# Swin block and dynamic depthwise convolution: the prologue of a long kernel reordered (raw means for folded weights, deviations between shift products, rows turned by DMA, zeroing on ScalarE)

## The chip, the cores and the metric

The kernel runs on one core of one Trainium2 chip. The metric is the device time of one run in microseconds, the median of several runs. Everything, prologue and weights included, happens in one launch.

## The reference, cut to what matters

Sixteen images of 192 channels and 56 x 56 pixels go through two layers. The first is a Swin block with shifted windows, the second a depthwise convolution whose taps are computed from the image's own channel means.

```python
# layer 0; x: (16, 192, 56, 56) float32, tokens are pixels
h = layernorm(x over channels) * norm1_g + norm1_b
h = roll(h, (-3, -3));  win = 7 x 7 windows of h          # 64 windows an image
q, k, v = win @ qkv_w + qkv_b                             # 192 -> 3 x 6 heads x 32
attn = softmax((q * 32**-0.5) @ k.T + rel_bias[REL_IDX] + mask)
x1 = x + roll_back((attn @ v) @ proj_w + proj_b)
y = layernorm(x1) * norm2_g + norm2_b
x2 = x1 + gelu(y @ fc1_w + fc1_b) @ fc2_w + fc2_b         # 192 -> 768 -> 192
# layer 1
t = relu(batchnorm(mean(x2 over pixels) @ w1.T))          # 192 -> 48
taps = (t @ w2.T + b2) * causal_mask                      # 4 taps a channel and image
out = depthwise3x3(x2, taps) + bias
```

## The kernel before, in words

**Tiles.** A step `i` is two window rows of an image, one from its upper and one from its lower half: 2 x 7 x 56 = 2 x 392 tokens. There are 4 steps an image and 64 in all. `x0` holds channels 0 to 127 of a whole image on 128 partitions; `x1` holds channels 128 to 191, the upper half of the image on partitions 0 to 63 and the lower on 64 to 127. An image is loaded already rolled.

**Layer norms without a mean.** The mean over channels is never subtracted from the tokens. The weights (`wqkv`, `wf1`) carry the norm's gamma and are centred instead, so that each output's weights add up to zero over the input channels; beta times the weights is added to the bias. A token is only multiplied by its inverse deviation, a *dv*. For that, `norm_squares` (L258) squares a step, `norm_stats` sums values and squares on TensorE (`st` in PSUM) with the selector `sel`, `norm_vars` and `norm_root` make variance and root, VectorE takes the reciprocal, and `norm_spread` (L350 on) writes the few rows to DRAM as `rows` and reads each back onto 128 partitions (`dv`, L366, on the SP queue). `norm1_scale` (L391, L399) multiplies and writes the windows `win`; `norm2_scale` (L413 to L419) does the same for the MLP's input `yn`. In the loop the stats come folded (`norm_folded`): two `xs` copies by DMA on SP bring halves side by side, GpSimd adds sums (L293, L295), squares are taken (L302, L309), and GpSimd adds the squares up (L314, L315).

**Attention of a step.** `attention_qk` makes `pq`, `pk` and `pe` and copies them out as queries `q4`, `q2` and as block-diagonal keys `kbd`, whose other entries stay zero from the prologue. `attention_v` makes `pv`; `attention_v_out` (L524) copies it into `vbd`, two buffers used in turn with zeros between heads, by block: half 0 by VectorE, half 1 by ScalarE. `attention_scores` gives, by window pair, `sc` on TensorE; `top` adds the table `bias_t` (L552, L559, position bias and mask) on VectorE and takes the exponent (L562) on ScalarE; `share` makes sums and quotients (L566 to L568, the last on GpSimd into `prob`). `attention_turn` transposes `prob` (`pt`, `prt`), `attention_values` gives `po`, `attention_rows` `o`, `project` `pp`, `residual` (L651, L657) adds it to `x`.

**The MLP.** `mlp_first` is fc1 and gelu (`ph`, L671), with callbacks `after` and `between` (the latter holds the `st` products of other steps); `mlp_wide`, `mlp_narrow` and `mlp_out` (L717) are fc2 (`pf`).

**Order.** Each engine executes what the program writes for it in that order[...]. PSUM is four pairs of banks, given out by hand with `banks(name, k)`. All matmuls go through the helper `mm` (L87). The loop body works on the convolution of an earlier image, the MLP of step `i-2`, the attention of step `i`, and queries and norms of later steps. Ahead of the loop a prologue (L853 to L1134) builds the weights and runs steps 0, 1 and part of 2 as pieces. All of the change lies in this prologue and in its helpers.

**The pieces of the prologue that the change touches**, in TensorE's order: `st_a` (stats of step 0), `fq_m` (means of the scaled qkv weights, by `fold_means`), `qkb_p` (`shift`: beta times the raw weights, one row), `dv` (step 0's two deviations spread by matmul), six one-row products that turn the `qkb` row into columns (`turn_row`), `st_b` (steps 1 and 2), step 0's `pq` to `pv`, scores `sc`, `pb_p` (fc1's shift row, turned by six more products, and small ones for the projection's bias), step 1's `pq`, and so on to `ff_m` (fc1's means), `st_c`, step 0's MLP and the loop. On VectorE: `fold_scale` (L158, L160) makes ten scaled copies of the qkv weights, `fold_center` subtracts the means, and `biases` (L911) builds four quarters of `bias_t`, 24 additions. On GpSimd and VectorE: the zeroing of `kbd`, `vbd` and `prob`. On SP: the loads of `x` and of the weights, one after the other.

Of the kernel before, what the change touches and what calls it, by code (L numbers as in the profile page):

```python
# [8 lines left out]
F32 = mybir.dt.float32  # L9
AF = mybir.ActivationFunctionType  # L10
ALU = mybir.AluOpType
# [8 lines left out]
N = WS * WS  # L20
# [16 lines left out]
def tile_swin_then_dynamic_conv(  # L37
# [48 lines left out]
    def mm(dst, lhs, rhs, start, stop):  # L86
        nc.tensor.matmul(dst, lhs, rhs, start=start, stop=stop, skip_group_check=True)  # L87
# [33 lines left out]
    def rows2(dst, src, queue):  # L121

        for h in range(2):
            queue.dma_start(dst[h * 64 : h * 64 + 64], src[C0:DIM])

    def columns_load(sources, tag, name, queue):
        n = sum(count for _, count in sources)
        rows = one.tile([n, 256], F32, tag=tag, name=f"{name}_rows")
        at = 0
        for src, count in sources:  # L130
            queue.dma_start(rows[at : at + count, 0:DIM], src.rearrange("(r c) -> r c", c=DIM))
            at += count
        return rows, n, name
# [17 lines left out]
    def fold_scale(raw, g, dst, groups, engine=nc.vector):  # L151
        for to, lo, n, factor in groups:
            for c in range(2):
                d, r = dst[:, c, to : to + n], raw[:, c, lo : lo + n]
                if engine is nc.scalar:
                    nc.scalar.activation(d, r, AF.Copy, scale=g[c])
                elif factor == 1.0:
                    nc.vector.tensor_scalar(d, r, g[c], None, ALU.mult)  # L158
                else:
                    nc.vector.tensor_scalar(d, r, g[c], factor, ALU.mult, ALU.mult)  # L160
# [15 lines left out]
    def shift(dst, raw, n, be, name):  # L176


        for c in range(2):
            cs = slice(c * n // 2, (c + 1) * n // 2)  # L180
            mm(dst[:, c, : n // 2], be[0].broadcast_to([128, 128]), raw[:, 0, cs], True, False)
            mm(
                dst[:, c, : n // 2],
                be[1][0:64].broadcast_to([64, 128]),
                raw[0:64, 1, cs],
                False,
                True,
            )
        row = one.tile([1, 2, n // 2], F32, tag="xs", name=name)
        nc.scalar.copy(row, dst[0:1, :, : n // 2])  # L190
        return row.rearrange("o c n -> o (c n)")

    def turn_row(dst, row, lo, n):
        mm(dst, row[:, lo : lo + n], ident[0:1, 0:1], True, True)
# [10 lines left out]
    qkb = const.tile([128, 3], F32, tag="qkb", name="qkb")  # L205
    wp0 = const.tile([128, DIM], F32, tag="wp0", name="wp0")
# [3 lines left out]
    f1b = const.tile([128, NFC], F32, tag="f1b", name="f1b")  # L210
    wf2 = const.tile([128, NFC, DIM], F32, tag="wf2", name="wf2")
# [27 lines left out]
    mask_t = one.tile([PW, 2, 2, N], F32, tag="prt", name="mask_t", bufs=4)  # L239
# [104 lines left out]
    def norm_vars(keys, st, tag="dev"):  # L344

        lo, hi = min(keys) * 32, max(keys) * 32 + 32
        d = one.tile([128, T], F32, tag=tag, name=f"dev_{keys[min(keys)]}")
        part = d[64 + lo : 64 + hi]
        nc.scalar.activation(part, st[lo:hi, 0, :T], AF.Square)
        nc.vector.tensor_tensor(part, st[64 + lo : 64 + hi, 0, :T], part, ALU.subtract)  # L350
        return part, d
# [4 lines left out]
    def norm_spread(keys, part, tags=("dv1", "sq01"), order=(1, 0)):  # L356

        rows = dram.tile([2 * len(keys), T], F32, tag="rows", name=f"rows_{keys[min(keys)]}")
        nc.sync.dma_start(rows, part[::16])
        out = {}  # L360
        for side in order:
            if side not in keys:
                continue
            v = one.tile([128, 2, T], F32, tag=tags[side], name=f"dv_{keys[side]}")
            at = 2 * (side - min(keys))
            nc.sync.dma_start(  # L366
                v,
                rows[at : at + 2].rearrange("(o h) t -> o h t", o=1).broadcast_to([128, 2, T]),
            )
            out[side] = v  # L370
        return out
# [61 lines left out]
    def attention_qk(i, kq, ke, kk, between=None, evac=nc.scalar, early=None, k_too=False):  # L433
# [34 lines left out]
        def biased(dst, src, b):  # L468
            if evac is nc.vector:
                nc.vector.tensor_scalar(dst, src, b, None, ALU.add)  # L470
            else:
                nc.scalar.activation(dst, src, AF.Identity, bias=b)

        def e(a):
            biased(q2[a * 64 : a * 64 + 64], pe[0:64, a, :T], qkb[0:64, 2:3])
            for h in range(2):
                p = slice(64 + h * HD, 64 + (h + 1) * HD)
                g = a * 2 + h
                biased(
                    kbd[g * HD : (g + 1) * HD, 2, :, h, :],  # L480
                    pe[p, a, :T].rearrange("p (w t) -> p w t", t=N),
                    qkb[p, 2:3],
                )
# [29 lines left out]
    def attention_v_out(pvs):  # L513

        for blk, pv in enumerate(pvs):
# [347 lines left out]
    for h in range(4):  # L863
        nc.vector.memset(pick[h * HD : (h + 1) * HD, h % 2 : h % 2 + 1], 1.0)
# [12 lines left out]
    load_rows(*images[0], 0, 3 * WS, HALF, nc.sync)  # L877
    nc.sync.dma_start(rawf[:, 0], fc1_w[0:C0])
    rows2(rawf[:, 1], fc1_w, nc.sync)
# [9 lines left out]
    nc.sync.dma_start(mask_t, win_mask)  # L889
# [15 lines left out]
    def biases(r, e):  # L905
        for half in range(2):
# [15 lines left out]
    nc.vector.memset(kbd, 0.0)  # L922
    norm_squares("1_0", 0, 0, nc.scalar, ("yn0", "q4"))
    fold_scale(
        raw,
        g1,
        wqkv,
        (
            (0, 0, 128, SCALE),
            (128, DIM, 128, 1.0),  # L930
            (256, 128, 64, SCALE),
            (320, DIM + 128, 64, 1.0),
            (384, 2 * DIM, DIM, 1.0),
        ),
    )
# [3 lines left out]
    part, _ = norm_vars(keys, st, "o")  # L939
    norm_root(part)  # L940
    nc.vector.reciprocal(part, part)
    norm_squares("1_1", 1, 0, nc.scalar)
    pm = fold_means(wqkv, 3 * DIM, "fq", 0)
    pq = banks("qkb_p", 2)
    row = shift(pq, raw, 3 * DIM, be1, "qkb_row")
    pq = pq[:, 0, 384:390]
    norm_squares("1_2", 2, 1, nc.scalar)

    pd = banks("dv_0", 3)
    for h in range(2):  # L950
        pick_row = ident[64:96, 64 + h * 16 : 65 + h * 16].broadcast_to([32, 128])
        mm(pd[:, h, :T], pick_row, part, True, True)
    fold_center(wqkv, 3 * DIM, pm)
# [8 lines left out]
    for _, c, at, lo, n, _ in parts:  # L962
        turn_row(pq[at : at + n, c : c + 1], row, lo, n)
    g2, be2, f2b, pb, cb = columns(*rows3, 1, nc.scalar.copy)
    norm1_scale(0, pd[:, :, :T], nc.vector)
    for dst, c, at, _, n, b in parts:
        nc.vector.tensor_tensor(dst, b, pq[at : at + n, c : c + 1], ALU.add)
    nc.vector.tensor_scalar(qkb[:, 0:1], qkb[:, 0:1], SCALE, None, ALU.mult)
    nc.vector.tensor_scalar(qkb[0:64, 2:3], qkb[0:64, 2:3], SCALE, None, ALU.mult)
    nc.vector.tensor_scalar(kb, pick, qkb[:, 1:2], None, ALU.mult)  # L970
# [4 lines left out]
    norm_stats(keys, {0: 1, 1: 2}, st)  # L975
    part, _ = norm_vars(keys, st)
    norm_root(part)
# [4 lines left out]
    for r in range(2):  # L982
        for e in range(2):
            biases(r, e)
# [11 lines left out]
    for t in (*vbd, *prob):  # L996
        nc.gpsimd.memset(t, 0.0)
# [9 lines left out]
    fold_scale(rawf, g2, wf1, ((0, 0, HID, 1.0),), nc.scalar)  # L1007
    norm1_scale(1, dvs.pop(0), nc.gpsimd)
    w2v = w2.rearrange("(c t) r -> c t r", t=9)[:, 0:NTAP, :]
    b2v = b2.rearrange("(c t) -> c t", t=9)[:, 0:NTAP]  # L1010
    nc.gpsimd.dma_start(w2n[:, 0], w2v[0:C0])
    nc.gpsimd.dma_start(b2t[:, 0], b2v[0:C0])
    rows2(w2n[:, 1], w2v, nc.gpsimd)
    rows2(b2t[:, 1], b2v, nc.gpsimd)
    nc.gpsimd.dma_start(wf2, fc2_w.rearrange("(f p) n -> p f n", p=128))
# [4 lines left out]
    pbp, f1p, pt = pv[:, 0, 384:386], pv[:, 0, 392 : 392 + NFC], pv[:, 1, 384:512]  # L1020
    top(0)
    row = shift(pv, rawf, HID, be2, "f1b_row")

    def rows_to_columns():
        for f in range(NFC):
            turn_row(f1p[:, f : f + 1], row, f * 128, 128)

    qs[1], outs = attention_qk(1, 2, 0, 1, rows_to_columns, nc.vector)
# [19 lines left out]
    share(3)  # L1048
    for c in range(2):
        nc.vector.tensor_tensor(pb[c], pb[c], pbp[:, c : c + 1], ALU.add)  # L1050
    nc.vector.tensor_tensor(f1b, f1b, f1p, ALU.add)
# [6 lines left out]
    outs[3]()  # L1058
    o = attention_rows(0, attention_values(0, prts, 3, 2))
# [16 lines left out]
    pm = fold_means(wf1, HID, "ff", 1)  # L1076
    top(2)
    residual(0, pp, pair1)
# [17 lines left out]
    dvs.update(norm_spread(keys, part))  # L1096
# [9 lines left out]
    v_whole()  # L1106
    copies, sums_, squares, fold = norm_folded("1_4", 4, 0)
    copies()
    squares(nc.scalar)()
    table(AF.Gelu)  # L1110
    sums_((0,))
    yns[0] = norm2_scale(0, dvs.pop(1), True)
    sums_((1,))
    fold()
    attention_v_out(pvs)
# [245 lines left out]
```

## Time and profile before

| | |
|---|---|
| median of 3 runs | 3045.67 us (3045.51 to 3046.77) |
| profiled run | 3046.2 us; span 3044.4 us |
| mean granted TensorE clock | 0.998 |
| TensorE busy | 3022.7 us of 3044.4, 25174 products |
| VectorE, ScalarE, GpSimd busy | 2156.3, 1948.7, 1343.5 us |
| span of the prologue on TensorE, first `st` product of the MLP at | 104.75 us |

PE is TensorE's matmul, PEld its weight load, DVE VectorE, ACT ScalarE, POOL GpSimd, SP the queue engine. TensorE is idle for some 22 us in all. A group's line reads: engine, operation, result<-operands, shape, count, then the time in brackets for which the engine stood idle ahead of it and what released it. Times at the left of a timeline are microseconds from the start of the span. Lines L87 are all matmuls, so they are told apart by the tile's name.

### The profile page before, as it was taken

How to read it: one execution, taken by the hardware profiler on the slowest of the kernel's cores; microseconds unless marked ns; L12 is line 12 of the kernel's file. 1: busy time of each engine (PE TensorE's matmuls, PEld its weight loads, DVE VectorE, ACT ScalarE, POOL GpSimd, SP SyncE). 2: the span in 40 equal slices, each digit the busy share in tenths (PEclk: the TensorE clock that was granted, in tenths of full speed). 3: DMA queues.
4: the chain of work that ended last, by engine and by line, in shares of the span. 5: the costliest groups of instructions: out<-in, count | busy, mean ns of one | idle time of the engine just before them, and what ended most of it. 6: DMA issues, size and time to landing. Idle time of an engine off the chain costs nothing.

```text
span 3044.4 us, 62149 instructions
## 1 busy us (share of the span) xinstructions
PE 3022.7 (99%) x25174; PEld 1891.4 (62%) x25174; DVE 2156.3 (71%) x3841; ACT 1948.7 (64%) x3159; POOL 1343.5 (44%) x1269
## 2 busy tenths in 40 slices
PE   9999999999999999999999999999999999999998
PEld 5666666666666666666666666666666666666654
DVE  8656677676686676776866867767767668668664
ACT  4666676666666666766766667667666667666563
POOL 6444534444435445344444444453454444444422
PEclk9999999999999999999999999999999999999999
DMA  4112121111211112121121211212111121211101
GB/s 111 33 31 59 41 75 41 43 60 46 73 38 62 52 44 68 44 72 36 41 67 47 70 36 52 65 41 78 39 47 56 46 73 38 62 52 43 33 30 56
DMA packets 68711, 159.89 MB, mean 53 GB/s; under 512 B 11250, under 2 KB 35288, under 8 KB 66504
## 3 DMA queue, kind: packets, MB, share of 16 engines
q1 hardware_dynamic: 66766, 153.84, 16.7%
q8 instruction: 199, 3.26, 0.4%
q0 software_dynamic: 1360, 1.26, 0.3%
q14 instruction: 88, 0.72, 0.1%
q10 hardware_dynamic: 298, 0.81, 0.1%
HBM read 92.24 MB, written 38.93 MB: 43 GB/s over the span
## 4 chain that ended last, share of the span: by engine, by line
PE 97%; DVE 1%; DMA 1%; POOL 1%; issue 0%; ACT 0%; SPq 0%; POOLq 0%; DVEq 0%; ACTq 0%
PE ph L87 26%; PE pf L87 25%; PE pv L87 8%; PE pp L87 8%; PE po L87 6%; PE pq L87 5%; PE pt L581 5%; PE sc L87 4%; PE pk L87 4%; PE pe L87 4%; PE st L87 2%; PE pc L87 0%; DMA wp<-in_L_conv_proj_w_dram 0%; PE pb_p L87 0%; DVE e L559 0%
## 5 line engine op out<-in xcount | busy, mean ns | idle before, releaser
L87 PE MATMUL pf<-hid,wf 128*128 128x392 f32 (+1 forms) x3072 | 802.6, 493 | 1.5 <-DVE e L552 1.5
L87 PE MATMUL ph<-yn,wf 128*128 128x392 f32 (+1 forms) x3072 | 799.3, 497 | 1.8 <-ACT vbd L524 1.5
L568 POOL TENSOR_TENSOR prob<-e,tot 113x588 f32<-113x588 f32 x256 | 298.3, 1176 | 1098.8 <-DVE tot L567 1098.6
L87 PEld LDWEIGHTS ph<-yn,wf 128*128 128x128 f32 (+1 forms) x3072 | 426.4, 188 | 346.6 <-issue 47.5
L87 PEld LDWEIGHTS pf<-hid,wf 128*128 128x128 f32 (+1 forms) x3072 | 386.2, 164 | 301.3 <-issue 120.2
L524 ACT COPY vbd<-pv 49x192 f32<-49x192 f32 x512 | 160.5, 313 | 575.9 <-DVE vbd L524 571.4
L717 DVE SCALAR_TENSOR_TENSOR x<-pf,cols,x 128x784 f32<-128x784 f32 (+1 forms) x128 | 106.2, 830 | 506.3 <-PE pf L87 447.6
L671 ACT ACTIVATE hid<-ph,f1b 128x784 f32<-128x784 f32 x384 | 337.2, 913 | 133.7 <-PE ph L87 132.2
L781 DVE SCALAR_TENSOR_TENSOR y<-x,wt,y 128x770 f32<-128x770 f32 x282 | 287.7, 1030 | 15.3 <-ACT y L773 7.0
L87 PEld LDWEIGHTS pv<-wqkv,win 64*128 64x128 f32 (+1 forms) x2048 | 255.4, 188 | 31.4 <-issue 1.2
L87 PE MATMUL pv<-wqkv,win 64*128 64x192 f32 (+1 forms) x2048 | 272.5, 325 | 0.3 <-DVE kbd L470 0.3
L559 DVE TENSOR_TENSOR e<-e,top 113x588 f32<-113x588 f32 x256 | 262.3, 1025 | 8.9
L293 POOL TENSOR_TENSOR xs<-x,x 64x392 f32<-64x392 f32 x246 | 249.1, 1013 | 34.4 <-DVE x L657 25.1
L87 PE MATMUL pp<-o,wp 128*128 128x392 f32 (+2 forms) x896 | 251.4, 514 | 0.0
L587 ACT COPY prt<-pt 128x678 f32<-128x678 f32 x256 | 179.2, 727 | 111.6 <-PE pt L581 110.1
L259 ACT ACT_TABLE_LOAD x192 | 246.3, 1283 | 5.3 <-issue 1.8
L562 ACT ACTIVATE e<-e 113x588 f32<-113x588 f32 x256 | 177.1, 692 | 109.7 <-DVE e L559 109.7
L552 DVE TENSOR_TENSOR e<-sc,bias_t 113x588 f32<-113x588 f32 x256 | 179.5, 762 | 60.6 <-PE sc L87 59.5
L415 POOL TENSOR_TENSOR yn<-x,dv 128x784 f32<-128x784 f32 x62 | 115.8, 1867 | 234.0 <-DMA dv<-rows 234.0
L581 PEld LDWEIGHTS pt<-ident,prob 113*128 113x128 f32 x1536 | 165.4, 141 | 64.9 <-issue 35.1
L87 PE MATMUL po<-prt,vbd 128*64 128x49 f32 x6144 | 196.8, 223 | 0.2 <-ACT prt L587 0.2
L87 PEld LDWEIGHTS po<-prt,vbd 128*64 128x64 f32 x6144 | 188.8, 138 | 9.4 <-ACT prt L587 0.5
(186 smaller groups left out, 4429.3 us busy)
## 6 DMA issues: line engine op xcount, KB each, us to landing
dv<-rows SPq DMA_DIRECT2D x127, 392.0 KB
xs<-x SPq DMA_DIRECT2D x246, 98.0 KB
x<-in_x_dram SPq DMA_DIRECT2D x15, 1484.0 KB
out_dram<-y SPq DMA_DIRECT2D x46, 392.0 KB
out_dram<-y SPq DMA_DIRECT2D x48, 196.0 KB
x<-in_x_dram SPq DMA_DIRECT2D x15, 392.0 KB
x<-in_x_dram SPq DMA_DIRECT2D x15, 350.0 KB
out_dram<-y SPq DMA_DIRECT2D x16, 308.0 KB
```

The source lines that it names most:

```text
L87: nc.tensor.matmul(dst, lhs, rhs, start=start, stop=stop, skip_group_check=True)
L259: nc.scalar.activation(junk, eps_t[0:1], func)
L293: nc.gpsimd.tensor_tensor(xs[p, 0], v0[p, h], v1[p], ALU.add)
L524: copy(dst, src[s * 64 : s * 64 + N, h, :, :, j, :])
L552: nc.vector.tensor_tensor(e, sc[:PW, :, : HEADS * N], rel, ALU.add)
L559: nc.vector.tensor_tensor(ehs[wp], ehs[wp], t.broadcast_to([PW, 2 * HEADS, N]), ALU.subtract)
L562: nc.scalar.activation(es[wp], es[wp], AF.Exp)
L568: nc.gpsimd.tensor_tensor(prob[wp][:PW, :, 0:N], ehs[wp], t.broadcast_to([PW, 2 * HEADS, N]), ALU.mult)
L581: nc.tensor.transpose(pt[:, a, g * PW : (g + 1) * PW], prob[wp][:PW, h : h + 2, :].rearrange("p h k -> p (h k)"), ident[:PW, :PW],)
L587: nc.scalar.copy(prt, pt[:, :, : 3 * PW])
L671: nc.scalar.activation(hid[:, f], phs[f][:, :, :T], AF.Gelu, bias=f1b[:, f : f + 1])
L781: nc.vector.scalar_tensor_tensor(dst, src, wt[:, kc, t : t + 1], dst, ALU.mult, ALU.add)
```

## The change

It rebuilds the first 100 us. Its parts, and what each is for:

1. *Means from the raw weights.* The means over channels are taken from `qkv_w` itself, with gamma divided by 192 (`gm`) as the stationary operand in place of a matrix of ones, so TensorE needn't wait for scaled weights. VectorE then makes weight and centring in one operation, raw times gamma minus mean. The query's scale moves from the weights to the keys' evacuation (`kbd`, `kb`).
2. *First deviations between shift products.* `dev_0` is a full zeroed tile, so step 0's deviations are picked with 128 rows in place of 32, and these products stand between the two halves of `shift`.
3. *Rows turned by transfers.* Six DMAs on SP carry the `qkb` row into the columns of `pq`, six more the fc1 row into `f1p`. `turn_row` is gone. The loads of fc1's weights and of step 3's rows of `x` go behind the first six; the mask's load comes earlier.
4. *Zeroing.* `kbd` and both `vbd` are zeroed by ScalarE (`clear`), `prob` by GpSimd behind step 1's windows.
5. *Half of the bias table later.* `biases(1, 0)` behind step 0's turns, `biases(1, 1)` in step 2's attention. The loads of `w2`, `b2` and fc2 go behind the `prob` of step 0.
6. *Order ahead of the loop.* `residual(0)` stands before `top(2)`. The deviation of the second norm is read back before that of the first, which is read only after `norm2_scale`. The copies into `vbd` of step 2 stand ahead of ScalarE's remaining squares of step 4.

```diff
+    def clear(t):
...
+        nc.scalar.activation(flat, ones[:, 0:1].broadcast_to(flat.shape), AF.Copy, scale=0.0)
...
-    def turn_row(dst, row, lo, n):
-        mm(dst, row[:, lo : lo + n], ident[0:1, 0:1], True, True)
...
-        nc.vector.memset(pick[h * HD : (h + 1) * HD, h % 2 : h % 2 + 1], 1.0)
+        nc.vector.memset(pick[h * HD : (h + 1) * HD, h % 2 : h % 2 + 1], SCALE)
...
-    load_rows(*images[0], 0, 3 * WS, HALF, nc.sync)
-    nc.sync.dma_start(rawf[:, 0], fc1_w[0:C0])
-    rows2(rawf[:, 1], fc1_w, nc.sync)
+    nc.sync.dma_start(mask_t, win_mask)
...
-    nc.vector.memset(kbd, 0.0)
+    gm = small.tile([128, 2, 1], F32, tag="gm", name="gm", bufs=1)
+    for c in range(2):
+        nc.vector.tensor_scalar(gm[:, c], g1[c], 1.0 / DIM, None, ALU.mult)
+    d0 = one.tile([128, T], F32, tag="o", name="dev_0")
+    nc.vector.memset(d0, 0.0)
     norm_squares("1_0", 0, 0, nc.scalar, ("yn0", "q4"))
-    fold_scale(
...
-    )
+    clear(kbd)
...
+    clear(vbd[0])
     nc.vector.reciprocal(part, part)
     norm_squares("1_1", 1, 0, nc.scalar)
-    pm = fold_means(wqkv, 3 * DIM, "fq", 0)
...
+            mm(m, gm[0:n, c].broadcast_to([n, 128]), r[0:n, c], c == 0 and k < 2, c == 1)
...
+            pick_row = ident[:, 64 + h * 16 : 65 + h * 16].broadcast_to([128, 128])
+            mm(pd[:, h, :T], pick_row, d0, True, True)
...
-        pick_row = ident[64:96, 64 + h * 16 : 65 + h * 16].broadcast_to([32, 128])
-        mm(pd[:, h, :T], pick_row, part, True, True)
-    fold_center(wqkv, 3 * DIM, pm)
+    row = shift(banks("qkb_p", 2), raw, 3 * DIM, be1, "qkb_row", first_deviations)
...
-        turn_row(pq[at : at + n, c : c + 1], row, lo, n)
+        nc.sync.dma_start(pq[at : at + n, c : c + 1], row[:, lo : lo + n])
+    nc.sync.dma_start(rawf[:, 0], fc1_w[0:C0])
+    rows2(rawf[:, 1], fc1_w, nc.sync)
+    load_rows(*images[0], 0, 3 * WS, HALF, nc.sync)
+    for c in range(2):
+        for m, d, r in groups:
+            nc.vector.scalar_tensor_tensor(d[:, c], r[:, c], g1[c], m, ALU.mult, ALU.subtract)
+    clear(vbd[1])
...
-    for r in range(2):
-        for e in range(2):
-            biases(r, e)
+    for e in range(2):
+        biases(0, e)
...
-    for t in (*vbd, *prob):
-        nc.gpsimd.memset(t, 0.0)
...
     norm1_scale(1, dvs.pop(0), nc.gpsimd)
...
+    for t in prob:
+        nc.gpsimd.memset(t, 0.0)
...
     row = shift(pv, rawf, HID, be2, "f1b_row")
...
-            turn_row(f1p[:, f : f + 1], row, f * 128, 128)
...
+    for f in range(NFC):
+        nc.sync.dma_start(f1p[:, f : f + 1], row[:, f * 128 : (f + 1) * 128])
...
+    biases(1, 0)
+    nc.vector.tensor_tensor(f1b, f1b, f1p, ALU.add)
     o = attention_rows(0, attention_values(0, prts, 3, 2))
...
+    residual(0, pp, pair1)
     top(2)
-    residual(0, pp, pair1)
...
-    dvs.update(norm_spread(keys, part))
+    read = norm_spread(keys, part, order=None)
+    dvs[1] = read(1)
...
+    biases(1, 1)
     copies, sums_, squares, fold = norm_folded("1_4", 4, 0)
     copies()
-    squares(nc.scalar)()
+    rest = squares(nc.scalar)
+    sums_((0,))
+    attention_v_out(pvs, (0,))
+    yns[0] = norm2_scale(0, dvs.pop(1), True)
+    dvs[0] = read(0)
+    attention_v_out(pvs, (1,))
+    rest()
     table(AF.Gelu)
-    sums_((0,))
-    yns[0] = norm2_scale(0, dvs.pop(1), True)
     sums_((1,))
     fold()
-    attention_v_out(pvs)
```

## The prediction, made before the changed kernel ran

> **What bounds the kernel now.** I read the page first: how full TensorE is, and how much of the last-ending chain is its own.
>
> ```profile
> PE 3022.7 (99%) x25174; PEld 1891.4 (62%) x25174; DVE 2156.3 (71%) x3841; ACT 1948.7 (64%) x3159; POOL 1343.5 (44%) x1269
> ...
> PE 97%; DVE 1%; DMA 1%; POOL 1%; issue 0%; ACT 0%; SPq 0%; POOLq 0%; DVEq 0%; ACTq 0%
> ```
>
> So a change pays only where TensorE waits, runs slowly, or loses an instruction. Every edit lies before the loop, so next I asked for TensorE's waits in the first 110 us:
>
> ```profile
> PE ph L87 <- ACT vbd L524: 1.5, 1, 1.5
> PE sc L87 <- ACT vbd L524: 1.4, 2, 0.7
> PE pq L87 <- POOL win L399: 0.9, 1, 0.9
> ```
>
> Above them stands only the wait for the first load (4.2 us), which nothing here touches; these three are 3.8 us. Then the clock, in windows of 3.4 us (columns: length, busy time of PE, PEld, DVE, ACT and POOL, granted clock, DMA share, GB/s):
>
> ```profile
> 13.70:17.10 3.40, 3.40 (x16) 1.75 (x15) 2.26 (x4) 1.45 (x3) 3.09 (x7) 1.00 1.09 262
> 17.10:20.50 3.40, 3.40 (x27) 1.97 (x30) 3.09 (x15) 0.52 (x2) 2.69 (x5) 0.50 0.75 141
> 20.50:23.90 3.40, 3.40 (x20) 1.17 (x14) 1.33 (x10) 0.56 (x2) 2.19 (x4) 0.50 0.40 44
> ```
>
> For 6.8 us the granted clock is 0.50: `st_b` steps every 0.65 us, its later twin `st_c` every 0.33. Last, the timeline around the first tile's attention and at the loop's start:
>
> ```profile
> 27.11 5.67 DVE L911 TENSOR_TENSOR bias_t<-rel_r,mask_t 113x98 f32<-113x98 f32 x24
> ...
> 28.82 0.82 SPq L366 DMA_DIRECT2D dv<-rows  x2
> ...
> 33.66 1.81 POOL L391 TENSOR_TENSOR win<-x,dv 128x343 f32<-128x343 f32 x2 [4.95 <-PE pv L87]
> ...
> 40.37 0.59 PE L87 MATMUL pq<-win,wqkv 64*128 64x392 f32 x1
> ```
> ```profile
> 92.22 0.53 ACT L302 ACTIVATE sq<-xs 128x392 f32<-128x392 f32 x1 [4.30 <-DMA xs<-x]
> ...
> 96.45 8.37 PE L87 MATMUL ph<-yn,wf 128*128 128x392 f32 x36 [1.53 <-ACT vbd L524]
> ...
> 103.33 1.18 POOL L315 TENSOR_TENSOR sq<-sq 128x392 f32<-128x392 f32 x1
> ...
> 104.75 0.11 PEld L87 LDWEIGHTS st<-xs,sel 128*32 128x32 f32 x2 [0.56 <-POOL sq L315]
> ```
>
> The reader should see two chains as long as TensorE's. The Pool (GpSimd) windows of tile 1 (33.66 to 39.4) end just before `pq` of tile 1. The Pool squares end at 104.51, just before `st`.
>
> **What the Trainium skill says.** *TensorE: Matmul & The Clock Gate*, Part 1 (the HAM clock gate): the clock halves after a window of 3413 ns with too little activity. The trace agrees: 6.8 us are two such windows, after small products (32-row `dv`, 1-row turns). *ScalarE: Activation LUTs*, "What ACT_TABLE_LOAD costs": 186 ns + 0.833 ns per element with immediate operands. The trace agrees: 784 elements took 0.86 us against 0.84. *DMA: Bandwidth & Descriptors*, "Anatomy of one DMA": about 2 us fixed, mostly the completion receipt. Here `rows` to the `dv` read that waits for it is 1.7 us, and an `xs` copy issued at 97.92 was waited for until 100.18, 2.26 us. *PSUM — Partial Sum Buffer*, "PSUM bank collisions": two engines may not touch one bank and quadrant together; so ScalarE's `vbd` copies of a block follow VectorE's (a 0.67 us wait at 34.37).
>
> **The change, part by part.** Times below are on the clock of the trace before.
>
> *Means from raw weights, one pass on VectorE.* Removed: 10 scalings (7.50 to 10.57), two centrings (1.42 us), the 2.02 us `kbd` memset. Added: six two-tensor operations over the same 1152 elements, about 1.8 us (the centrings' 1.42 plus overhead for four more). The chain `st_a` to reciprocal is unchanged and still ends at 14.45, so VectorE has `wqkv` at 16.3, starts windows of tile 0 at 16.5 instead of 17.23 and ends at 19.6. On TensorE the means take about 2.1 us instead of 2.86, since they change row mode once, not per half.
>
> *Deviations on all 128 rows between shift products.* The first shift half ends at 13.4, `dv` must wait for the reciprocal until 14.5, the second half ends at 17.25. This fills the window that was thin before. `st_b` then needs 2.0 us at full clock, 4.0 at half; `pq` of tile 0 starts at 19.7 or 21.5 instead of 22.55. I take full; the next parts make it matter little.
>
> *Zeroing on ScalarE.* By the price above: `kbd` (2352) 2.15 us, each `vbd` (1536) 1.47 us. ScalarE was idle 3.86 us before 10.07, which hides `kbd`. The others sit ahead of the squares of tiles 1 and 2 (end 15.95, needed 17.25) and of `st_b`'s square (19.45, needed 19.9): nothing.
>
> *The row turned by transfers.* Removed: 1.8 us of tiny products here and 1.43 at 43.17. Added: six transfers on the SP queue. The row exists at 18.0; issues of about 0.55 us and a landing time of 2.2 put the last column at 23.0 (bounds: 1.7 after the last issue, 22.5; double overhead, 24.5). Behind the six adds VectorE queues tile 1's reciprocal: it ends at 26.1 instead of 27.08. Behind the six issues SP queues fc1 (768 KB), the last tile's rows (588 KB), then `rows`. Nine issues and that data fill SP until 26.6; `rows` lands near 29, and `dv` is issued at 29, not earlier than the 28.82 before. It took until at most 33.66 there; I take 33.0 to 33.9. So Pool's windows start where they did, within 0.7 us.
>
> *Half of the bias table deferred.* 12 operations of 0.236 us leave the chain; with the reciprocal's 1 us, the last score product moves from 37.18 to about 33.4. The other halves lie in VectorE's idle stretches (2.56 us before 57.11, 3.63 before 90.94) at 1.42 us each: nothing.
>
> *Sum at tile 1's `pq`.* TensorE arrives at 37.5, Pool ends at 38.8 to 39.6: a new wait of 1.3 to 2.1 us. From there to `pt` is 7.65 us (9.87 less 1.43 of turns, less 0.8 of overlap with `pb_p`): 46.85 instead of 50.24. Gain 3.4. The `prob` memsets (2.8 us) behind the windows end near 42.0 and the last `prob` by 47.4; `pt` needs it at 49: hidden. The w2 transfers follow, where Pool idles.
>
> *`residual(0)` before `top(2)`.* The exponent of pair 2 now ends at 71.3 instead of 69.2; queued behind it on ScalarE are the squares for `st_c`, which slip from 71.85 to 72.6. `st_c` waited for them: loss 0.55.
>
> *The loop's start.* ScalarE now copies `vbd` before the squares of tile 4, so `ph` starts 1.53 us earlier. But those squares end near 96.7 instead of 93.7, and Pool's L314 (94.74 before) waits. From L314 to the end of L315 Pool needs 9.3 us (9.77 less a 0.49 wait): 106.0 instead of 104.51. TensorE reaches `st` at 102.85 and waits 3 us. Net: loss 1.3 where 1.5 was to be won.
>
> Sum: 3.4 - 0.55 - 1.3 = 1.5 us. After 110 us TensorE has no wait that the change touches. Forecast 3045.67 - 1.5 = 3044.2.
>
> **Rivals.**
> A: `dv` lands by 32 (SP drains sooner) and the squares fold without a wait, because `dv` of side 1 is read alone. Gain 4.9 - 0.55 + 1.5 = 5.9, at most 6.4 without the ScalarE slip: about 3039.5. For it: 784 KB moved for the two reads together. Against: Pool's 9.3 us stays.
> B, the other side: the new 3 us wait at `st` makes a thin window, so one more window of 3.4 us runs at half clock (cost 1.7), and the single-element transfers cost double (1 to 2 more). 1.5 - 1.7 - 1.5 = -1.7: 3047.4. For it: the window from 13.7 was nearly continuous and still lost the clock. Against: from 34.1 to 37.6 TensorE was busy only 2.11 of 3.50 us and kept it.
> C: only the first half works (no wait at `st`, `dv` as forecast): 3.4 - 0.55 + 1.5 = 4.4, 3041.3.
>
> **How the numbers follow.** Forecast 0.42, C 0.20, A 0.16, B 0.18, something worse (transfers of several us each holding tile 1's reciprocal) 0.04. The 0.2% bound is 6.1 us, so faster means below 3039.6: half of A and a little of C, 0.12. Slower means above 3051.8: only the last, 0.04. Same: 0.84. The range goes from A's end, 3039.2, to B with late transfers, 3048.2.
>
> **What would show it.** Right: six pq transfers landing near 23; clock 1.00 from 17 to 24; `dv` issued near 29; tile 1's `pq` waiting for Pool 1 to 2 us; `ph` with no wait, `st` waiting about 3 us for L315's successor. Wrong: `dv` issued by 27, or L314 not waiting for ScalarE (gain above 4), or a clock of 0.50 after `st` (loss).

## The result, and the profile after

| | median | runs | ratio to before |
|---|---|---|---|
| before | 3045.59 us (3044.54 to 3047.28) | 6 | |
| changed | 3055.95 us (3053.73 to 3058.28) | 6 | 1.0034, 95% interval 1.0021 to 1.0047 |

The change costs 10.4 us (6.4 to 14.3 by the interval); forecast was a gain of 1.5. TensorE is still full (3026.8 us busy of 3055.0, was 3022.7 of 3044.4), so the question is where in the first 120 us it lost its place. The table sets the starts of TensorE's groups in the two timelines against each other:

| TensorE reaches | before | after | lag |
|---|---|---|---|
| `st_b` | 18.47 | 16.04 | -2.43 |
| `pq`, tile 0 | 22.55 | 18.74 | -3.81 |
| scores, tile 0 | 33.83 | 29.79 | -4.04 |
| `pb_p` | 37.84 | 38.79 | +0.95 |
| `pt`, tile 0 | 50.24 | 52.77 | +2.53 |
| `st_c` | 72.17 | 75.51 | +3.34 |
| `pe` behind `st_c` | 74.28 | 79.28 | +5.00 |
| `ph`, first | 96.45 | 99.76 | +3.31 |
| `ph` behind `st` | 105.55 | 113.80 | +8.25 |
| scores, tile 2 | 109.70 | 119.44 | +9.74 |

The start gained 3.81 us at tile 0's `pq` (forecast 2.85) and 4.04 at the scores. About 0.5 of it is chance: the first load, which the change doesn't touch, ended TensorE's first wait at 3.69 us where it was 4.17. Then the gain was lost in four places: at the scores (5.0), up to `pt` (1.6), from there to `pe` (2.5, of which 1.66 in `st_c` alone), and at `st` (4.9, and 1.5 in the `ph` behind it). Only the `vbd` wait ahead of `ph` paid back 1.7. From the projection of step 2 to that of the last step the lag grows from 9.74 to 10.82 in a few small steps, whose causes are not known.

The view of waits in the first 115 us of the changed kernel (engine, line, what it waited for; total, times, longest):

```profile
POOL win L393 <- DMA dv<-rows: 15.4, 1, 15.4
...
POOL sq L314 <- ACT sq L309: 4.9, 1, 4.9
DVE cols L993 <- DMA pq<-qkb_row: 4.7, 2, 4.4
ACT kbd L468 <- DVE kb L995: 4.3, 1, 4.3
...
PE sc L87 <- ACT kbd L474: 2.5, 2, 1.4
PE st L87 <- POOL sq L315: 2.3, 1, 2.3
...
PE sc L87 <- ACT vbd L528: 2.2, 2, 2.0
```

Two chains can be read off. VectorE waits for a transferred column, ScalarE's keys wait for VectorE's `kb`, TensorE's scores wait for the keys. And GpSimd waits for ScalarE's squares, TensorE's `st` for GpSimd. The first of them in VectorE's timeline (start, length, what ran, and in brackets the idle time ahead with what ended it):

```profile
22.61 0.16 DVE L993 TENSOR_TENSOR cols<-cols,pq 128x1 f32<-128x1 f32 x1 [0.30 <-DMA pq<-qkb_row]
27.15 0.15 DVE L993 TENSOR_TENSOR cols<-cols,pq 64x1 f32<-64x1 f32 x1 [4.38 <-DMA pq<-qkb_row]
27.31 0.15 DVE L994 TENSOR_SCALAR qkb<-qkb 64x1 f32<-64x1 f32 x1
27.48 0.23 DVE L995 TENSOR_SCALAR kb<-pick,qkb 128x2 f32<-128x2 f32 x1
27.74 2.60 DVE L998 RECIPROCAL dev<-dev 64x392 f32<-64x392 f32 x1
```

The sixth column holds 64 of the 192 values of v's shift, which nobody needs before 51 us. But VectorE runs in order: behind its addition stand `kb` and tile 1's reciprocal. The reciprocal's operand had been ready since 20.41, when ScalarE's root ended; it still ran only behind the addition, and ends at 30.3 instead of 27.1. The SP queue's timeline goes on from there:

```profile
16.80 4.47 SPq L976 DMA_DIRECT2D pq<-qkb_row  x6
21.32 0.59 SPq L977 DMA_DIRECT2D raw<-in_L_conv_fc_w_dram  x1
...
28.91 0.47 SPq L113 DMA_DIRECT2D x<-in_x_dram  x1
30.36 0.60 SPq L360 DMA_DIRECT2D rows<-dev  x1
32.58 0.80 SPq L365 DMA_DIRECT2D dv<-rows  x2
```

`dv` is issued at 32.58 (28.82 before), so GpSimd's windows of tile 1 start at 36.75 (33.66 before; there they waited for tile 0's `pv`, which reads the one `win` that they overwrite, and not for `dv`). What the scores' waits do next is in the windows of 3.4 us (columns as in the prediction; TensorE's busy time is the second figure, the granted clock the third from the end):

```profile
17.10:20.50 3.40, 3.10 (x29) 1.62 (x22) 2.07 (x12) 2.41 (x5) 3.40 (x7) 1.00 0.28 34
20.50:23.90 3.40, 3.40 (x13) 1.80 (x10) 0.47 (x3) 2.33 (x3) 0.82 (x2) 1.00 0.79 24
...
30.70:34.10 3.40, 1.24 (x32) 0.88 (x32) 3.34 (x14) 2.43 (x5) 0.00 (x0) 1.00 0.24 70
34.10:37.50 3.40, 1.28 (x26) 0.95 (x24) 3.28 (x8) 2.45 (x8) 0.75 (x1) 0.62 0.68 204
37.50:40.90 3.40, 3.29 (x27) 1.95 (x28) 2.77 (x5) 1.82 (x3) 3.25 (x5) 0.50 1.00 424
40.90:44.30 3.40, 3.40 (x6) 1.01 (x6) 3.30 (x7) 0.69 (x1) 3.11 (x10) 0.50 1.02 232
44.30:47.70 3.40, 3.40 (x16) 1.99 (x13) 1.77 (x4) 1.97 (x3) 3.15 (x4) 0.87 0.29 62
```

The clock from 17 to 24 us is 1.00, as forecast. But TensorE is busy for 1.24 and 1.28 us of the two windows from 30.7, and the clock is 0.50 from 35 to 45. Seven `pb_p` products take 5.74 us, where before they took 3.11 (first line before, second after):

```profile
37.84 3.11 PE L87 MATMUL pb_p<-raw,cols 128*128 128x384 f32 x7
...
38.79 5.74 PE L87 MATMUL pb_p<-raw,cols 128*128 128x384 f32 x7
```

The same happens after the waits at 73 (`st_c`) and at 111 (`ph`).

The second chain, in ScalarE's timeline ahead of the loop:

```profile
92.37 0.55 ACT L302 ACTIVATE sq<-x 128x392 f32<-128x392 f32 x1
96.39 1.33 ACT L528 COPY vbd<-pv 49x192 f32<-49x192 f32 x4 [3.47 <-DVE vbd L528]
99.97 1.33 ACT L528 COPY vbd<-pv 49x192 f32<-49x192 f32 x4 [2.24 <-PE pp L87]
101.32 0.53 ACT L302 ACTIVATE sq<-xs 128x392 f32<-128x392 f32 x1
101.76 1.05 ACT L309 ACTIVATE sq<-x 64x392 f32<-64x392 f32 x2
```

ScalarE stands idle for 5.7 us while squares that it could take are queued behind two groups of `vbd` copies, which wait for VectorE's. (The view names TensorE's `pp` for the second. VectorE's second group ended at 99.86 too, 0.1 us ahead of ScalarE's, and the same distance separates the two engines' copies in the other steps.) GpSimd's fold (L314 to L315 of both halves) starts at 102.89 and ends at 112.81; TensorE had reached `st` at 108.33. The last line is the kernel before, where the same twelve `ph` products took 4.22 us:

```profile
108.33 0.85 PE L87 MATMUL st<-xs,sel 128*32 128x392 f32 x2
...
112.87 1.00 PE L87 MATMUL st<-sq,sel 128*32 128x392 f32 x2 [2.35 <-POOL sq L315]
113.80 5.71 PE L87 MATMUL ph<-yn,wf 128*128 128x392 f32 x12
...
105.55 4.22 PE L87 MATMUL ph<-yn,wf 128*128 128x392 f32 x12
```

### The profile page after: what moved, and what is told of

Same layout as the page of the kernel before. It is cut to its first block, busy times and chain, and to the rows that moved or that the text cites. A ratio compares the mean times of both kernels' runs of the same rounds, so it can differ in the third digit from the quotient of the medians.

```text
span 3055.0 us, 62120 instructions
## 1 busy us (share of the span) xinstructions
PE 3026.8 (99%) x25154; PEld 1892.2 (62%) x25154; DVE 2161.6 (71%) x3836; ACT 1954.0 (64%) x3162; POOL 1343.5 (44%) x1267
## 4 chain that ended last, share of the span: by engine, by line
PE 97%; DVE 2%; POOL 1%; DMA 1%; issue 0%; ACT 0%; SPq 0%; ACTq 0%; POOLq 0%; DVEq 0%
PE ph L87 25%; PE pf L87 25%; PE pv L87 8%; PE pp L87 8%; PE po L87 6%; PE pq L87 5%; PE pt L585 5%; PE sc L87 4%; PE pk L87 4%; PE pe L87 4%; PE st L87 2%; PE pc L87 0%; PE pb_p L87 0%; DMA pq<-qkb_row 0%; DVE e L563 0%
## 5 line engine op out<-in xcount | busy, mean ns | idle before, releaser
L293 POOL TENSOR_TENSOR xs<-x,x 64x392 f32<-64x392 f32 x246 | 249.7, 1015 | 33.7 <-DVE x L661 24.5
```

What stands on the lines that cost most here:

```text
L293: nc.gpsimd.tensor_tensor(xs[p, 0], v0[p, h], v1[p], ALU.add)
```

## The experiments

All are edits of the changed kernel, except `f8`. Ratios are to the kernel before, measured on the same chip; its median lay between 3045.56 and 3046.33 there. The changed kernel itself was timed in six runs only, beside the first row of the table above, so its 3055.95 is good to a few microseconds. `e1`, `e2`, `e3` and `h3` have five or six runs each, and their intervals overlap its own: what these four show, they show in their timelines and not in their time. One profile stands for each kernel, and profiles of one kernel can part, as some below do.

**First set: which part costs.**

`e1`, the qkb row turned by products again, behind `st_b`:

```diff
-        nc.sync.dma_start(pq[at : at + n, c : c + 1], row[:, lo : lo + n])
...
+        mm(pqp[at : at + n, c : c + 1], row[:, lo : lo + n], ident[0:1, 0:1], True, True)
```

> The changed kernel, but the qkb row is turned by six one-row products again (behind st_b), not by transfers. Theory 'held queue': the sixth transfer landed at 27.15 us, and VectorE's add for it held kb (so ScalarE's kbd, so the scores) and tile 1's reciprocal (so rows, dv, GpSimd's windows); then here kb is ready by 22, the reciprocal ends near 23 to 25 instead of 30.3, pb_p starts at 34 to 36 instead of 38.8 and keeps full clock, pt starts near 47 to 49 instead of 52.8: about 3051, 4 to 6 us under the changed kernel's 3056. Rival 'thin windows': the loss is TensorE's halved clock at st_c and at the loop's st, which the row doesn't touch: pt comes early here, but the time stays within 2 us of 3056. Rival 'more products': the six products cost 1.8 us and give nothing back: 3057 or more.

Measured 3055.28 us, 1.0030 (1.0018 to 1.0041). The held queue was real: the reciprocal ended at 25.8, `dv` was issued at 28.22. But the early start was spent before it helped: six products, a wait of 0.9 us for `pe`'s banks, and half clock from 23 to 27; the scores came at 34.39, later than in the kernel before. GpSimd's windows started only at 34.22, held again by tile 0's `pv` and not by `dv`. `pt` was 3.2 us earlier than in the changed kernel, the time only 0.7. So the numbers of "thin windows" were met and those of "held queue" were not. Of the two places that "thin windows" named, the half clock came at the loop's `st` (112 us) and not at `st_c`; in this trace it came at 23 and 51 us as well.

`e2`, the two v columns added behind the bias table:

```diff
-    for dst, c, at, _, n, b in parts:
+    for dst, c, at, _, n, b in parts[:4]:
         nc.vector.tensor_tensor(dst, b, pq[at : at + n, c : c + 1], ALU.add)
...
+    for dst, c, at, _, n, b in parts[4:]:
+        nc.vector.tensor_tensor(dst, b, pq[at : at + n, c : c + 1], ALU.add)
```

> The changed kernel with its transfers, but VectorE adds the two v columns (the last two transfers) behind the reciprocal and the bias table. Theory 'held queue': kb is ready at 22.9 instead of 27.7, the scores run from 29.5 on without a wait for kbd, and the reciprocal ends by 25.6; but rows stays behind the loads of fc1 and x on SP until about 29, so GpSimd's windows move by only about 1 us and tile 1's pq takes the wait over: 3053 to 3056. Rival 'the order alone': if only the scores' delay counted, 4 us: 3052 or less. Rival 'thin windows': no change, 3056.

3055.60 us, 1.0031 (1.0019 to 1.0043). `kb` was ready at 22.6 and `pb_p` started at 33.35, 5.4 us earlier. All of it was lost at the next wait, tile 1's `pq`, and in the half clock from 38 to 48: `rows` was still behind the loads (28.55), `dv` was issued only at 31.64, and GpSimd's windows started 1.2 us earlier than in the changed kernel. TensorE's waits:

```profile
PE pq L87 <- POOL win L401: 6.7, 2, 5.8
```

So the late column is one of two delays in a row, and curing it alone moves the wait, as "held queue" had it.

`e3`, the loads of fc1 and x issued behind `dv` (three lines moved):

> The changed kernel, but the loads of fc1 (768 KB) and of the last rows of x (588 KB) are issued behind rows and dv, not in front of them. Theory 'loads delay the column': the sixth transfer was still in flight when the loads' packets filled the DMA engines, so here it lands by 23, tile 1's reciprocal ends near 26, dv lands near 31 instead of 36.7, pt starts at 46 to 48: 3048 to 3052. Rival 'single elements are slow by themselves': the sixth column still lands at 25 or later, and the gain is the queue's alone, 1 to 2 us: 3054 to 3055.

3057.33 us, 1.0034 (1.0022 to 1.0047). The last two columns were added at 22.83 to 23.13 and GpSimd's windows started at 32.15, as expected. But now fc1 came late: ScalarE waited 2.36 us for it, and TensorE was busy for 1.34 and 1.77 us of the two windows from 30.7, after which the clock was 0.50 until 44. `pt` came at 50.88 instead of 46 to 48.

`e4`, the old order ahead of the loop:

```diff
-    dvs[1] = read(1)
+    dvs.update(norm_spread(keys, part))
...
-    rest = squares(nc.scalar)
-    sums_((0,))
-    attention_v_out(pvs, (0,))
-    yns[0] = norm2_scale(0, dvs.pop(1), True)
-    dvs[0] = read(0)
-    attention_v_out(pvs, (1,))
-    rest()
+    squares(nc.scalar)()
     table(AF.Gelu)
+    sums_((0,))
+    yns[0] = norm2_scale(0, dvs.pop(1), True)
     sums_((1,))
     fold()
+    attention_v_out(pvs)
```

> The changed kernel, but the order ahead of the loop is the old one: both second-norm reads at once, ScalarE's squares of tile 4 before its vbd copies. Theory 'squares held GpSimd': in the changed kernel GpSimd's L314 waited 4.93 us for ScalarE's squares, and TensorE's st products came 4.7 us late and the next ph ran 1.5 us longer at half clock; here ph waits some 1.5 us for vbd again and st waits at most 1 us: 3050.5 to 3052, 4 to 5.5 us under 3056. Rival 'the lag only moves': the wait is the fold's own length and comes back at ph or st: within 1.5 us of 3056.

3050.85 us, 1.0015 (1.0008 to 1.0021): 5.1 us of the loss, inside "squares held GpSimd". No run of it (at most 3053.08) reaches the changed kernel's fastest (3053.73). L314 started at 96.60 without a wait, and TensorE did not wait at `st`.

**Second set: the same two causes, cured instead of undone.** `f5` moves one call:

```diff
     sums_((0,))
+    rest()
     attention_v_out(pvs, (0,))
...
     attention_v_out(pvs, (1,))
-    rest()
```

> The changed kernel, with one call moved: ScalarE's remaining squares of tile 4 stand ahead of the first vbd copies, in the 3.5 us in which ScalarE waited for VectorE there; the reads stay split and vbd still comes before the Gelu table. Theory 'squares held GpSimd': L314 no longer waits 4.93 us, st comes without a wait and keeps full clock, and ph starts without its old wait for vbd: 6 us under the changed kernel, 3049 to 3050.5, at or below the old loop start's 3050.85. Rival 'split reads': if the later read of the first norm's dv or VectorE's vbd split held the loop, st still waits 2 us or more and the time stays above 3053.

3049.61 us, 1.0010 (1.0003 to 1.0016). ScalarE's timeline ahead of the loop:

```profile
90.99 0.54 ACT L302 ACTIVATE sq<-x 128x392 f32<-128x392 f32 x1
93.89 0.53 ACT L302 ACTIVATE sq<-xs 128x392 f32<-128x392 f32 x1 [2.36 <-DMA xs<-x]
94.33 1.05 ACT L309 ACTIVATE sq<-x 64x392 f32<-64x392 f32 x2
95.40 1.33 ACT L528 COPY vbd<-pv 49x192 f32<-49x192 f32 x4
```

The squares now fill the gap. GpSimd's fold runs from 96.50 to 107.47, `ph` starts without a wait, and `st` to the next `ph` takes 1.39 us instead of 5.47. The split reads and the early `vbd` copies are still in place, so they were no fault; one call's place was.

`f6` puts fc1's loads in SP's idle time behind `mask_t`, the rows of x behind `dv`, and the v columns as in `e2`.

> The changed kernel with its transfers, but fc1's loads are issued ahead of them (in SP's idle 9.8 to 16.8 us), the last rows of x behind dv, and the two v columns are added behind the bias table. Theory 'held queue' (queue and contention together): kb by 23, scores end near 33.4, dv is issued near 27 and lands by 31.5, GpSimd's windows end near 37, tile 1's pq waits under 1.5 us and the clock stays at 1.00 through 38 to 48; pt starts at 45.5 to 47.5 where it was 52.8: 3050 to 3051.5. Rival 'any early start turns into waiting': TensorE waits for GpSimd's windows and the half clock comes all the same, pt at 50 or later: 3053.5 or more.

3050.24 us, 1.0013 (1.0006 to 1.0019). Windows started at 31.60, tile 1's `pq` at 37.55 without a wait, `pt` at 46.11:

```profile
30.70:34.10 3.40, 1.32 (x54) 1.01 (x48) 3.30 (x7) 3.01 (x9) 2.50 (x3) 1.00 0.95 296
34.10:37.50 3.40, 3.40 (x20) 1.24 (x12) 3.25 (x6) 1.95 (x3) 3.06 (x9) 1.00 1.01 375
37.50:40.90 3.40, 3.40 (x14) 1.64 (x14) 3.33 (x6) 1.73 (x3) 3.30 (x5) 1.00 1.03 270
```

`f7` is both edits together.

> Both edits before this one together (queue order and v columns, squares first). If the two causes are the whole loss and add up: 3055.95 less 5 less 6, 3044 to 3045.5, at or a little under the kernel before; if the early start is worth the 4 us that the forecast gave it, 3041 to 3043. Rival 'lost elsewhere': a new thin window at st_c or at pt takes 1.7 us a time, 3047 or more.

3045.05 us, 0.9996 (0.9988 to 1.0004). From the changed kernel's 3055.95, `f5` took 6.3 and `f6` 5.7, and both together 10.9, which is the whole loss. That is 1.1 less than the sum of the two, within what six runs of the changed kernel leave open. The code of `f6` and `f7` is the same up to 90 us, and yet here the clock fell:

```profile
30.70:34.10 3.40, 0.99 (x36) 0.80 (x40) 3.30 (x8) 2.79 (x9) 2.23 (x3) 1.00 0.96 294
34.10:37.50 3.40, 3.40 (x28) 1.17 (x19) 3.29 (x5) 2.02 (x3) 3.09 (x9) 0.58 1.02 376
37.50:40.90 3.40, 3.40 (x9) 1.69 (x10) 3.16 (x6) 0.24 (x2) 3.27 (x7) 0.50 1.05 278
```

With 1.32 us of work in a window one profile kept its clock, with 0.99 the other lost it; `pt` came at 46.11 and 48.73.

`f8` is the kernel before with only the new order ahead of the loop.

> The kernel before, with nothing of the change but its order ahead of the loop (split reads, vbd copies ahead of ScalarE's remaining squares). Theory 'squares held GpSimd': about 5 us slower than before by itself, 3050 to 3052, with L314 waiting 4 to 5 us. Rival 'it needs the late prologue': within 1.5 us of before, 3045 to 3047.5.

3050.23 us, 1.0013 (1.0007 to 1.0020). L314 waited 3.62 us for ScalarE. The new order is slow by itself, by 3.9 us. This profile shows something else. Up to the new order, at 83 us, its code is that of the kernel before, with the same 32-row and one-row products, and the clock that was 0.50 from 17 to 24 us there is 1.00 here:

```profile
13.70:17.10 3.40, 3.40 (x20) 2.11 (x19) 2.49 (x5) 1.80 (x3) 3.35 (x7) 1.00 1.12 272
17.10:20.50 3.40, 3.31 (x33) 1.47 (x32) 3.17 (x19) 0.66 (x2) 2.23 (x4) 1.00 0.59 120
20.50:23.90 3.40, 3.40 (x16) 1.75 (x15) 2.68 (x6) 2.20 (x4) 3.24 (x5) 1.00 0.81 46
```

Its `pt` came at 47.86 (50.24 in the profile before). So the half clock there isn't fixed by the products, and some of what the table of lags shows is the state of one profile.

**Third set: what is left.** `g1` is `f7` with tile 1's reciprocal ahead of the additions that wait for columns.

> The run with both edits (queue order, squares first), and tile 1's reciprocal ahead of the additions that wait for the turned row, so that VectorE's 2.9 us of waiting for transfers is filled. If what is queued behind the transfers' columns on VectorE is what the early start lacks: rows leaves at 22.7 instead of 26.4, GpSimd's windows start at 28 to 29 instead of 31.9, VectorE's vbd copies some 2 us earlier, the scores end near 32.5, tile 1's pq waits under 1 us, the clock holds from 34 to 42, pt starts at 43.5 to 46: 3040 to 3042.5. Rival 'ScalarE is the bound': the scores' waits for vbd stay at 2.9 us in all, the clock drops as there, 3044 or more.

3044.17 us, 0.9994 (0.9986 to 1.0002). A miss: `rows` left at 22.97, but the read of it only at 27.89:

```profile
16.70 4.88 SPq L978 DMA_DIRECT2D pq<-qkb_row  x6
22.97 0.59 SPq L360 DMA_DIRECT2D rows<-dev  x1
27.89 0.80 SPq L365 DMA_DIRECT2D dv<-rows  x2
```

So the windows still started at 32.03, tile 1's `pq` waited 2.0 us, and the clock was 0.50 from 38 to 41.5. ScalarE was not the bound either: the scores' waits fell from 2.9 to 1.2 us.

`g2` is `g1` with `top(2)` ahead of `residual(0)`.

> The run before this one, with top(2) ahead of residual(0) again, as in the kernel before. The forecast charged the new order 0.55 us (ScalarE's squares for st_c queued behind a later exponent): the stretch from the first pt of step 0 to the first pt of step 1 is 30.2 to 30.6 us with the new order where the clock held, and 29.6 with the old; here 29.6, and the time 0.5 to 0.9 us lower. Rival: the order costs nothing and the stretch differs by the clock's windows alone: within 0.3 us of the run before.

3044.31 us, 0.9993 (0.9984 to 1.0001), within 0.3 us of `g1`, as the rival had it. The stretch between the `pt`s was 30.49 us, and 29.67 in `g1`, the wrong way round for a cost: the order of the residual costs nothing that shows.

`g3` picks the deviations from 32 rows behind both halves of `shift`, in the changed kernel.

```diff
-    row = shift(banks("qkb_p", 2), raw, 3 * DIM, be1, "qkb_row", first_deviations)
+    row = shift(banks("qkb_p", 2), raw, 3 * DIM, be1, "qkb_row")
...
+        pick_row = ident[64:96, 64 + h * 16 : 65 + h * 16].broadcast_to([32, 128])
+        mm(pd[:, h, :T], pick_row, part, True, True)
```

> The changed kernel with step 0's deviations picked from 32 rows, behind both halves of shift, as in the kernel before. Theory 'few rows make a thin window': the clock is 0.50 for one or two windows of 3.4 us between 16 and 24, st_b takes 4.0 us instead of 2.0, tile 0's pq starts at 20.5 or later. Rival 'the one-row products made it': those are gone here too, so the clock stays at 1.00 from 17 to 24 and pq starts within 0.5 us of 18.7. The whole time within 3 us of 3056 in both.

One run, 3049.42 us. The clock stayed at 1.00 from 13.7 to 23.9 and tile 0's `pq` started at 18.25: 32 rows did not cost the clock here. As `f8`'s profile keeps the clock with the one-row products too, `g3` can't say that those made the half clock before. And the row left at 15.46, the last column was added at 22.50.

`h2` is the same kernel, timed.

> The single look at deviations from 32 rows, timed. If the place of the deviations (0.7 us of waiting for the reciprocal between the halves of shift, and the row later by 1.3 us) is what tips the last columns into the following loads: 3049 to 3051.5, 5 us or more under the changed kernel, with the last column added by 23. Rival 'one lucky look': the last column comes at 26.5 or later, and the median is within 2 us of 3056.

3052.07 us, 1.0020 (1.0013 to 1.0027): 3.9 us under the changed kernel, between the two expectations; its slowest runs (3056.37) lie among the changed kernel's. The last column was added at 20.73, and at 22.50 in `g3`'s profile of the same kernel. Either way it came before the column of the changed kernel; whether the place of the deviations or the earlier row does this is not shown. The squares still held `st` (2.35 us).

`h3`, GpSimd's loads of `fc1_b` and of the batch norm's rows issued behind the zeroing of `prob`.

> The changed kernel, with GpSimd's loads of fc1_b (768 single elements) and of the four batch-norm rows (128 partitions each) issued behind the prob zeroing instead of at 17 to 21 us. Rival to the loads of fc1 and x as what delays the columns: if these small packets are it, the last column is added by 23.5 and the time falls to 3049 to 3052. If fc1's and x's data are it, the column still comes at 26 or later: 3054 to 3056.5.

3057.26 us, 1.0037 (1.0024 to 1.0049). The columns left 1.1 us later than in the changed kernel and yet the last was added at 23.9, with fc1's and x's loads in place. In the profiles of `e4` and `f5`, whose code is the changed kernel's there, it came at 26.7 and 27.25, as late as in its own. So small loads look like part of what delays a column, as the large ones do (`e3`), each by one profile. Only the column was cured, and as in `e2` the wait moved to `pq` (3.4 us, and half clock from 41 to 48). The times in this expectation were wrong.

`h1` joins the edits of `g2` and `g3`.

> The run with the old residual order (all four edits), and step 0's deviations from 32 rows behind both halves of shift. The single look at those deviations had no half clock from 16 to 24 and the row 1.3 us earlier on SP (15.5 instead of 16.8). If the earlier row empties the DMA engines sooner: rows to dv takes under 3 us instead of 4.6 to 4.9, dv is issued by 26, GpSimd's windows start by 30, tile 1's pq waits under 1 us, pt starts by 45: 3041 to 3043.5. Rival 'the wait is the transfers' own': rows to dv takes 4 us or more again and the time stays within 1 us of 3044.3.

3043.66 us, 0.9994 (0.9985 to 1.0002). `rows` to `dv` still takes 4.45 us, as the rival had it. In its trace `pt` starts at 45.04, the clock is 1.00 from 10 to 119 us, and scores of tile 2 come 5.7 us earlier than in the profile of the kernel before; but `f8`'s profile, with the old front and no half clock there, was itself 2.4 us ahead of that one at `pt`. The medians differ by 1.9 us, and the interval includes no difference: the change can be mended to the old time, and a gain beyond it isn't established.

## Why the prediction was wrong

*Front of the kernel: right, part of it for a wrong reason.* `st_b` came at 16.04 (forecast 17.25), tile 0's windows ended at 18.5 (19.6), `pq` at 18.74 (19.7), the clock was 1.00. The forecast laid the old half clock on small products (32 rows, one row). `g3` and `h2` have the 32 rows and keep the clock, and `f8`'s profile keeps it with all of the old products. So the change can't be credited with the clock, and what took it in the profile before stays open. Placing the deviations between the halves of `shift` brought a wait of 0.74 us for the reciprocal (1.1 forecast), and the row left at 16.80 where it left at 15.46 in `g3`.

*Zeroing on ScalarE: right.* It took 2.15 us for `kbd` and 1.48 for each `vbd`, hidden; the estimate from the Trainium skill, *ScalarE: Activation LUTs*, "What ACT_TABLE_LOAD costs", was 2.15 and 1.47.

*The row turned by transfers: the first step that failed.* "The last column at 23.0", 24.5 at most: it was 27.15. The issues took 0.75 us each, not 0.55, but that isn't it: the row left at 16.80 (forecast 18.0), and the last issue began at 19.95 where the forecast's sum has 20.75. From there the landing took 7.2 us (5.9 from the end of the issue), not 2.2. The skill's fixed cost of about 2 us (*DMA: Bandwidth & Descriptors*, "Anatomy of one DMA", given there for transfers that GpSimd issues) isn't a bound here: these transfers, issued by SP, are hundreds of single elements in company with other loads. `e3`, `h3` and `h2` each thin the company or leave ahead of it, and each has the column by 24. What in the company holds the elements up was not separated.

*What waits behind it: half named.* The forecast put the reciprocal behind the additions but not `kb`, and so not ScalarE's keys and the scores, the last of which it had at 33.4; it came at 37.6. And it issued `dv` at 29 where it was 32.58, as `rows` waited for the reciprocal and for SP's loads. That step would have failed with the column on time as well: in `e2` and `h3` `rows` left at 28.55 and 27.49 (forecast 26.6), `dv` could be issued only 3.1 and 3.6 us later, at 31.64 and 31.05, and tile 1's `pq` waited 5.8 and 3.4 us where 1.3 to 2.1 was forecast. In the changed kernel the wait stood at the scores instead, 5 us. The forecast did write down "transfers of several us each holding tile 1's reciprocal", at a chance of 0.04. The reciprocal was held; the transfers were issued in time and landed late.

*Residual order: 0.55 us forecast, nothing seen* (`g2`).

*The loop's start: right mechanism, wrong size, one term missing.* `ph` started 1.7 us sooner (forecast 1.5). The squares ended later than forecast, since ScalarE's second `vbd` copies wait for VectorE's, which stand behind `norm2_scale`, and the fold took 9.92 us, not 9.3. `st` to `ph` took 4.7 us more, where 3 were forecast. And the half clock afterwards, 1.5 us, stood only in rival B. Why ScalarE's copies follow VectorE's is open: the forecast named the rule of PSUM banks, but in the kernel's code the copies of one block read the two different banks of a pair.

*The clock.* The sum priced each wait at its length. In the trace three thin stretches were followed by 10, 3.4 and 3.4 us at half clock, some 2.6 us in `pb_p`, 1.66 in `st_c` and 1.5 in `ph`. Rival B had one of them, and so the range's end of 3048.2 was far too low. That thin windows bring the half clock fits most profiles and not all: the profile before lost the clock behind a window filled for 3.40 of 3.40 us, and `f6` kept it with 1.32. No run set it by itself, so that stays argued.

## What to carry to other kernels

Before an operation on the chip is replaced by small transfers, list what stands behind each consumer on every in-order queue, and give the result that nobody needs soon its own, later place. Then look at the next wait in the same way: moving the late column alone gave no time (`e2`), together with the loads on SP it gave about 6 us (`f6`). A wait of TensorE in a part of small products can cost more than its length, since the clock may fall after it: in the changed kernel a wait of 1.0 us ahead of `st_c` was followed by 3.4 us at half clock, which cost 1.66. When an engine's order is changed to serve one consumer sooner, look for the idle time ahead of that work and fill it first with what the others wait for: moving one call was worth 6 us here, as much as the other repairs together.

## What the runs showed of the hardware that was not expected

In the changed kernel a transfer of 64 to 128 single elements to as many partitions held the SP queue for 0.53 to 1.33 us. The last of six was there 5.9 us after the end of its issue, and 1.7 and 3.3 us in the two profiles of one kernel in which the row left earlier (`h2`, `g3`). A read that needed `rows` (6 KB) could be issued 1.7 us after the write in `f6`, where the DMA engines were then busy for at most a tenth of the time, 2.2 to 3.6 us after it where the loads of fc1 and x had just been issued (the changed kernel, `e2`, `h3`), and 4.4 to 4.9 us after it when the six transfers had just been issued (`g1`, `g2`, `h1`). The clock's fall is not fixed by the program: `f6` and `f7`, alike up to 90 us, kept and lost it at the same place, and reached `pt` 2.6 us apart; the kernel before and `f8`, alike up to 83 us, differ in the same way from 17 to 24 us, and by 2.4 us at `pt`, of which about 0.5 lies ahead of the fall.
